# An LSTM inside a two-layer kernel: one tile and one transpose per gate, direct sigmoid and tanh, the cell as a scan, and work around it moved

## The chip, the cores and the metric

The kernel runs on one core of a Trainium2 chip. Its time is the device time of one execution in microseconds, shown as the median of several runs. One execution more was taken with the hardware profiler. The engines are named as the profile names them: PE (TensorE matmuls), PEld (its weight loads), DVE (VectorE), ACT (ScalarE), POOL (GpSimd) and SP (SyncE, which only issues DMAs here). All data is fp32.

## The reference

Two layers, each of an attention-like block and a feed-forward-like block with residual additions, on x of 8 sequences (B) of 512 steps (S) and 256 features (D). The first layer's second block begins with an LSTM, whose outputs go into a routed attention. What the change touches is this LSTM, with H = 256 and all 8 sequences run side by side:

```python
xW = jnp.einsum('ntd,dg->ntg', x, Wx) + b          # 256 -> 4 * 256
def step(carry, xw_t):
    prev_h, prev_c = carry
    a = xw_t + prev_h @ Wh
    i = jax.nn.sigmoid(a[:, :Hdim])
    f = jax.nn.sigmoid(a[:, Hdim:2 * Hdim])
    o = jax.nn.sigmoid(a[:, 2 * Hdim:3 * Hdim])
    g = jnp.tanh(a[:, 3 * Hdim:])
    next_c = f * prev_c + i * g
    next_h = o * jnp.tanh(next_c)
    return ((next_h, next_c), next_h)
```

The states h of all steps are kept, and their mean over the steps enters a router. Other blocks used below: the first layer's attention with a sum over 32768 edges (the "edge stage"); its gated output ("gating"), which makes the LSTM's input x; and "adaptive weights", a product of a hidden vector with a 256 x 8192 matrix for the second layer.

## The kernel before

**Stages.** In order of time: attention of the first layer, the edge stage (to about 446 us), the LSTM loop (464 to 1695 us), routed attention, the second layer's attention, and a second recurrence (a plain tanh RNN, L1419 to L1440) with a mixture of experts beside it.

**One LSTM step** (`lstm`, from L599, the loop from L669). States are kept transposed: features on 128 partitions, two halves k, 8 sequences, so that h is a 128x8 stationary operand. The 1024 gate columns are laid out by the host (`gates`) as four blocks j of 256, each of 64 columns for i, f, g, o. Block j's product lands on partitions 32j to 32j+7 of PSUM tiles: `pgi` (64 columns of i and 64 of f), `pgg` and `pgo`, each in two buffers that alternate by step.

- PE, L677: for each of the three tiles 8 matmuls (2 halves x 4 blocks) add h Wh to what the tile holds.
- PE, L657 (`seed`): right behind them, 12 matmuls put xW of the next step into the other buffers: the stationary operand picks 8 rows of `xw`, a 128x1024 tile of 16 steps x 8 sequences.
- DVE, L683 and L687: three 32x32-block transposes of PSUM tiles into `G`, of 128, 64 and 64 columns.
- ACT, L684 and L688: tanh of i and f together, of g, of o. Sigmoid is written as a tanh: the weights and the bias of i, f and o are halved beforehand (L592 to L595), h is kept doubled, and the cell doubled as well; the DVE operations and the scale of the last tanh make up for it:

```python
STT(pr[:, 1], X[:, 1], 1.0, X[:, 3], ALU.add, ALU.mult)
STT(pr[:, 0], X[:, 0], 1.0, X[:, 2], ALU.add, ALU.mult)
STT(X[:, 3], pr[:, 1], 0.5, pr[:, 0], ALU.mult, ALU.add)
nc.scalar.activation(th, X[:, 3], AF.Tanh, scale=0.5)
STT(ring[:, t % RB], to, 1.0, th, ALU.add, ALU.mult)
```

These are L690, L691, L693 (DVE), L695 (ACT) and L696 (DVE). L696 writes h of the step into `ring`, a tile of 8 steps with two buffers. The next step's L677 waits for it.

**Work between the steps.** The loop is under a manual schedule: PE, ACT and DVE execute in the order in which the code issues, POOL and SP are placed by the scheduler. Behind each step, by its position `at` = t mod 16, a piece of other work is issued:

- `rest`, the generator `gating` (L523 to L553), one of its 8 pieces in positions 15 and 0 to 6. It makes x of 16 steps for a later chunk: two matmuls to `pv` and an addition (L534, L535) in positions 15 and 0, two copies with bias on ACT and two additions (L538, L539) in 1, then products, a tanh and a square (L542, L544, L545, L547, L549), and the result (L552) in 6. `pv` is a single PSUM buffer of the pool `a_pv`.
- `extra`, the generator `adaptive_weights` (L1071 to L1090), in positions 1, 2, 3: a matmul to `pw`, a second one, then the addition of a 8x512 row (L1088) and the DMA of the result. There are 16 rounds of three pieces, in the first 16 chunks. `pw` uses the same PSUM buffer as `pv`. SP loads weights and bias rows ahead (L1080, L1082).
- `project` (L634 to L648): from position 6, two copies on POOL (L639), then eight matmuls (L645) and four additions (L647) give `xw` of the next chunk, through one PSUM buffer.
- every 8 steps: a sum over the 8 states (L708, DVE) and, on POOL, L709, the copy of the 8 states to `hT` times 0.5.

**Before the loop.** In the edge stage (`Edges.sums`), for each of 32 groups DVE makes one-hot tiles (L457, L477) and PE multiplies with them (L468, transposes L485, L489). After its second group `lstm_weights` loads Wx, Wh and the bias (Wh on ACT's queue) and scales them on DVE (L592 to L595); the groups 4, 6 and 8 each let gating take a piece. Then six more pieces follow (L573), then the first `project`, the first seed and the loop. Router (L774): the mean of h with the factor 0.5 / S.

Of the kernel before, what the change touches and what calls it, by code (L numbers as in the profile page):

```python
# [509 lines left out]
def l0_attention(K, es, states):  # L510
# [44 lines left out]
    with ExitStack() as e1:  # L555
# [8 lines left out]
        with ExitStack() as e2:  # L564
            enc0 = K.pool(e2, "a_wv").tile([P, 2, S], F32, name="enc0")
            nc.vector.tensor_tensor(enc0, denseT[:, :, 0, :], xgT, ALU.add)
            with tc.manual_schedule(engines=ORDERED):
                for g, _ in enumerate(edges.sums(enc0, e2, alpha)):
                    if g == 1:
                        weights = lstm_weights(K, lw)  # L570
                    if g in (4, 6, 8):
                        next(rest)
    for _ in range(6):  # L573
        next(rest)
    return hT, rest, weights, pp

# [4 lines left out]
def lstm_weights(K, wp):  # L581

    nc, inp = K.nc, K.inp

    wx = load_kp(nc, wp, inp["lstm_wx"], "wx", 1024)
    wh = load_kp(nc, wp, inp["lstm_wh"], "wh", 1024, eng=nc.scalar)
    bias = wp.tile([P, 1024], F32, name="bias")
    nc.sync.dma_start(out=bias, in_=inp["lstm_b"].partition_broadcast(P))
    for t, f, fg in ((wx, 0.5, None), (bias, 0.5, None), (wh, 0.25, 0.5)):
        t5 = t if t is bias else t.rearrange("p k n -> p (k n)")  # L590
        t5 = t5.rearrange("p (j g n) -> p j g n", g=4, n=64)
        nc.vector.tensor_scalar(t5[:, :, 0:2, :], t5[:, :, 0:2, :], f, None, ALU.mult)  # L592
        nc.vector.tensor_scalar(t5[:, :, 3, :], t5[:, :, 3, :], f, None, ALU.mult)
        if fg is not None:
            nc.vector.tensor_scalar(t5[:, :, 2, :], t5[:, :, 2, :], fg, None, ALU.mult)  # L595
    return wx, wh, bias


def lstm(K, hT, rest, weights, extra):  # L599

    nc, inp = K.nc, K.inp
    ident, xT = K.ident, K.xT  # L610
    mm = nc.tensor.matmul
    STT = nc.vector.scalar_tensor_tensor
    XB = GT
    RB = 8
    with ExitStack() as es:
        wp = K.pool(es, "l_w")
        sp = K.pool(es, "l_s", 3)
        rp = K.pool(es, "l_r", 2)
        xp = K.pool(es, "l_xw", 2)
        psx = K.pool(es, "l_px", 1, PSUM)  # L620
        psg = K.pool(es, "l_pg", 1, PSUM)
        wx, wh, bias = weights
        h0 = wp.tile([P, 2, B], F32, name="h0")
        nc.vector.tensor_scalar(h0, K.h0T, 2.0, None, ALU.mult)
        pick = ident.rearrange("p (b t) -> p t b", b=B)

        pgi = [psg.tile([P, 2, 64], F32, name=f"pgi{i}") for i in range(2)]
        pgg, pgo = [[psg.tile([P, 64], F32, name=f"{n}{i}") for i in range(2)] for n in ("pgg", "pgo")]
        for t in (*pgi, *pgg, *pgo):
            nc.vector.memset(t, 0.0)  # L630
        X = sp.tile([P, 4, 2, B], F32, name="X", tag="X")
        nc.vector.memset(X[:, 3], 0.0)

        def project(t0):  # L634

            xw = xp.tile([P, 1024], F32, name="xw", tag="xw")
            xc = xp.tile([P, 2, P], F32, name="xc", tag="xc")
            for k in range(2):
                nc.gpsimd.tensor_copy(xc[:, k].rearrange("p (b t) -> p b t", b=B), xT[:, k, :, t0 : t0 + XB])  # L639
            yield xw  # L640
            for n in range(4):
                c = slice(n * 256, n * 256 + 256)
                px = psx.tile([P, 256], F32, name="px", tag="px")
                for k in range(2):
                    mm(px, xc[:, k], wx[:, k, c], start=(k == 0), stop=(k == 1))  # L645
                    if k == 1:
                        nc.vector.tensor_tensor(xw[:, c], px, bias[:, c], ALU.add)  # L647
                    yield  # L648

        def parts(t):  # L650

            return (pgi[t % 2], 0, 128), (pgg[t % 2], 128, 192), (pgo[t % 2], 192, 256)

        def seed(t, xw):
            for dst, lo, hi in parts(t):
                for j in range(4):
                    mm(dst[32 * j : 32 * j + B], pick[:, t % XB, :], xw[:, j * 256 + lo : j * 256 + hi], start=True, stop=False)  # L657

        proj = project(0)
        xw = next(proj)  # L660
        for _ in proj:
            pass
        proj = iter(())
        nxt = None
        ring = None
        seed(0, xw)
        E = mybir.EngineType
        es.enter_context(K.tc.manual_schedule(engines={E.PE, E.Activation, E.DVE}))
        for t in range(S):  # L669
            if t % RB == 0:  # L670
                last = ring
                ring = rp.tile([P, RB, 2, B], F32, name="ring", tag="ring")
            for dst, lo, hi in parts(t):
                for k in range(2):
                    hp = h0[:, k, :] if t == 0 else (ring[:, t % RB - 1, k] if t % RB else last[:, RB - 1, k])
                    for j in range(4):
                        mm(dst[32 * j : 32 * j + B], hp, wh[:, k, j * 256 + lo : j * 256 + hi], start=False, stop=(k == 1))  # L677
            if t + 1 < S:
                if t % XB == XB - 1:
                    xw = nxt  # L680
                seed(t + 1, xw)
            G = sp.tile([P, 4, 2, 32], F32, name="G", tag="G")
            nc.vector.transpose(G[:, 0:2].rearrange("p g k b -> p (g k b)"), pgi[t % 2].rearrange("p g n -> p (g n)"))  # L683
            nc.scalar.activation(X[:, 0:2], G[:, 0:2, :, 0:B], AF.Tanh)  # L684
            to = sp.tile([P, 2, B], F32, name="to", tag="to", bufs=2)
            for g, ps, th in ((2, pgg[t % 2], X[:, 2]), (3, pgo[t % 2], to)):
                nc.vector.transpose(G[:, g].rearrange("p k b -> p (k b)"), ps)  # L687
                nc.scalar.activation(th, G[:, g, :, 0:B], AF.Tanh)  # L688
            pr = sp.tile([P, 2, 2, B], F32, name="pr", tag="pr")
            STT(pr[:, 1], X[:, 1], 1.0, X[:, 3], ALU.add, ALU.mult)  # L690
            STT(pr[:, 0], X[:, 0], 1.0, X[:, 2], ALU.add, ALU.mult)  # L691
            X = sp.tile([P, 4, 2, B], F32, name="X", tag="X")
            STT(X[:, 3], pr[:, 1], 0.5, pr[:, 0], ALU.mult, ALU.add)  # L693
            th = sp.tile([P, 2, B], F32, name="th", tag="th")
            nc.scalar.activation(th, X[:, 3], AF.Tanh, scale=0.5)  # L695
            STT(ring[:, t % RB], to, 1.0, th, ALU.add, ALU.mult)  # L696
            at = t % XB
            if at < 7 or at == XB - 1:
                next(rest, None)
            if 0 < at < 4:  # L700
                next(extra, None)
            if at == 6 and t - 6 + XB < S:
                proj = project(t - 6 + XB)
                nxt = next(proj)
            elif at > 6:
                next(proj, None)
            if t % RB == RB - 1:
                nc.vector.tensor_reduce(K.hpart[:, t // RB], ring.rearrange("p t k b -> p k b t"), AX.X, ALU.add)  # L708
                nc.gpsimd.tensor_scalar(  # L709
                    hT[:, :, :, t - RB + 1 : t + 1], ring.rearrange("p t k b -> p k b t"), 0.5, None, ALU.mult  # L710
                )
        for _ in extra:
            pass

# [32 lines left out]
def routed_heads(K, hT, T):  # L747
# [4 lines left out]
    with ExitStack() as es:  # L752
# [18 lines left out]
        for k in range(2):  # L771
            mm(pl, hsum[:, k, :], wr[:, k, :], start=(k == 0), stop=(k == 1))
        lg = wp.tile([B, NH], F32, name="lg")
        nc.vector.scalar_tensor_tensor(lg, pl, 0.5 / S, br, ALU.mult, ALU.add)  # L774
        nm = wp.tile([B, 1], F32, name="nm")
        sm = wp.tile([B, 1], F32, name="sm")
        nc.vector.tensor_reduce(nm, lg, AX.X, ALU.max, negate=True)
# [293 lines left out]
def adaptive_weights(K, wd, hT, pp):  # L1071

    nc, inp = K.nc, K.inp
    mm = nc.tensor.matmul
    with ExitStack() as es:
        sp = K.pool(es, "d_s", 2)
        for n in range(16):
            c = slice(n * S, (n + 1) * S)
            w2 = sp.tile([P, 2, S], F32, name="w2")
            nc.sync.dma_start(out=w2, in_=inp["ada_w2"][:, c].rearrange("(k p) n -> p k n", p=P))  # L1080
            b2 = sp.tile([B, S], F32, name="b2")
            nc.sync.dma_start(out=b2, in_=inp["ada_b2"][c].partition_broadcast(B))  # L1082
            pw = pp.tile([P, S], F32, name="pw", tag="pv")[0:B, :]
            for k in range(2):
                mm(pw, hT[:, k, :], w2[:, k, :], start=(k == 0), stop=(k == 1))
                yield
            ws = sp.tile([B, S], F32, name="ws")
            nc.vector.tensor_tensor(ws, pw, b2, ALU.add)  # L1088
            nc.sync.dma_start(out=wd[:, c], in_=ws)
            yield  # L1090


class Attention:
# [764 lines left out]
def two_layers_kernel(tc, *args):  # L1858
    inp, out = dict(zip(NAMES, args)), args[-1]
    with ExitStack() as es:  # L1860
        K = State(tc, inp, es)
        with tc.tile_pool(name="wd", bufs=1, space=DRAM) as dp, ExitStack() as eh:
# [11 lines left out]
            with ExitStack() as e0:  # L1874

                adaptive_hidden(K, gT)
                hT, rest, weights, pp = l0_attention(K, e0, states)
                lstm(K, hT, rest, weights, adaptive_weights(K, wd, gT, pp))
            el.close()
            with ExitStack() as e1:  # L1880
                T = Layer1(K, e1, wd)
# [19 lines left out]
def lay_out(i):  # L1901
# [10 lines left out]

    def gates(w):
        w = w.reshape(w.shape[:-1] + (4, 4, 64))
        return w[..., [0, 1, 3, 2], :, :].swapaxes(-2, -3).reshape(w.shape[:-3] + (1024,))

    def rank_major(w):
        w = w.reshape(w.shape[:-1] + (4, D, 8)).swapaxes(-1, -2)
# [99 lines left out]
```

## Time and profile before

| | |
|---|---|
| median of 10 runs | 4071.5 us (4061.75 to 4076.65) |
| the profiled execution | 4066.82 us, span of its instructions 4065.0 us |
| mean granted clock of TensorE | 0.967 |
| busy share of the span | PE 87%, PEld 60%, DVE 58%, ACT 37%, POOL 15% |
| LSTM loop, first to last h | 464.55 to 1694.76 us, 511 intervals, mean 2.407 us |
| matmuls in a step | 24 of h Wh, 12 of the seed; each shows as two in the trace |

How to read it: times are counted from the span's start. PE's busy share counts matmuls whose ends are modelled and which overlap, so a high share does not say that PE is full. A line such as "ACT X L684 <- DVE G L683: 658.9, 511, 2.3" says that ACT's instruction of line 684 stood idle for DVE's of line 683: in total, how often, the longest. In a timeline a bracket gives the idle time ahead of an instruction and what released it. Lines are those of the kernel before.

### The profile page before, as it was taken

To read this page: it belongs to the slowest core of one execution; us is meant where nothing else is said; L and a number is where in the kernel's file an instruction comes from. 1 tells how busy PE (TensorE), PEld (TensorE's weight loads), DVE (VectorE), ACT (ScalarE), POOL (GpSimd) and SP (SyncE) were. 2 spreads that over 40 slices of the span, in tenths; PEclk is the share of its full clock that TensorE was granted. 3 is DMA by queue.
4 is the path that set the end of the run, shared out by engine and by line. 5 is a ranking of instruction groups with operands and counts; after the bars stand their busy time and mean duration, and the time that the engine had idled before them with its cause. 6 is when DMAs were issued, how large, how long until landed. Compare 5 with 4: busy or idle time off the path is not lost.

```text
span 4065.0 us, 150864 instructions
## 1 busy us (share of the span) xinstructions
PE 3516.3 (87%) x65188; PEld 2440.4 (60%) x65188; DVE 2350.3 (58%) x8838; ACT 1509.0 (37%) x5341; POOL 606.4 (15%) x1250
## 2 busy tenths in 40 slices
PE   8999888888878888599988999999998797999884
PEld 5533466666666666466656666666666565767564
DVE  4488566666666666467656666666666433333332
ACT  3111233333333333255544444444444322333242
POOL 1010000000000000111022222222222121030412
PEclk9899999999999999899999999999999997999897
DMA  3111000000000000200000000000000122443476
GB/s 106 43 67 69 23 21 21 15 21 15 5 4 4 4 4 4 76 25 25 1 2 2 1 1 2 1 2 1 1 1 1 36 75 69 125 149 102 133 246 202
DMA packets 104842, 173.14 MB, mean 43 GB/s; under 512 B 12576, under 2 KB 71872, under 8 KB 103792
## 3 DMA queue, kind: packets, MB, share of 16 engines
q1 hardware_dynamic: 79792, 114.23, 9.0%
q0 software_dynamic: 12064, 34.34, 2.5%
q10 hardware_dynamic: 12320, 14.94, 1.1%
q8 instruction: 511, 8.37, 0.9%
q14 instruction: 155, 1.27, 0.1%
HBM read 124.53 MB, written 40.10 MB: 40 GB/s over the span
## 4 chain that ended last, share of the span: by engine, by line
PE 44%; DVE 6%; ACT 4%; DMA 2%; issue 1%; SPq 0%; ACTq 0%; POOL 0%; DVEq 0%; POOLq 0%
PE pg L1435 5%; PE pe L1231 4%; PE pt L1274 3%; PE pp L1191 3%; PE po L1289 3%; PE pg L1657 3%; PE px L1306 3%; ACT sm L1251 2%; PE pv L1211 2%; DMA x<-xs 2%; PE pe L893 2%; PE pp L869 1%; PE po L930 1%; PE pt L915 1%; PE py L1673 1%
## 5 line engine op out<-in xcount | busy, mean ns | idle before, releaser
L677 PE MATMUL pgi<-wh,ring 128*8 128x128 f32 x8176 | 325.3, 274 | 209.7 <-DVE ring L696 209.2
L677 PEld LDWEIGHTS pgi<-wh,ring 128*8 128x8 f32 x8176 | 173.9, 89 | 377.2 <-DVE ring L696 366.1
L684 ACT ACTIVATE X<-G 128x32 f32<-128x32 f32 x512 | 117.3, 229 | 671.9 <-DVE G L683 671.9
L1440 DVE STREAM_TRANSPOSE ring<-h 128x64 f32<-128x64 f32 x512 | 125.5, 245 | 396.3 <-ACT h L1439 383.3
L1251 ACT ACTIVATE sm<-sm,nm 128x388 f32<-128x388 f32 (+3 forms) x512 | 284.0, 556 | 175.6 <-DVE nm L1247 175.2
L683 DVE STREAM_TRANSPOSE G<-pgi 128x128 f32<-128x128 f32 x512 | 161.9, 316 | 258.8 <-PE pgi L677 258.7
L1439 ACT ACTIVATE h<-pg 128x64 f32<-128x64 f32 x512 | 114.2, 223 | 456.8 <-PE pg L1435 420.8
L1191 PE MATMUL pp<-hn,wqkv 128*128 128x512 f32 x512 | 243.1, 619 | 30.7 <-ACT oT L1290 29.8
L1435 PE MATMUL pg<-wh,ring 128*8 128x64 f32 x8176 | 221.8, 229 | 52.8 <-DVE ring L1440 49.6
L1274 PE MATMUL pt<-ident,sm 128*128 128x128 f32 x1280 | 191.2, 281 | 75.3 <-DVE sm L1257 62.6
L1274 PEld LDWEIGHTS pt<-ident,sm 128*128 128x128 f32 x1280 | 147.9, 143 | 157.5 <-issue 96.1
L1276 ACT COPY eT<-pt 128x512 f32<-128x512 f32 (+1 forms) x192 | 105.4, 549 | 346.8 <-PE pt L1274 345.4
L1258 POOL COPY pme<-sm 128x4 f32<-128x4 f32 x512 | 119.7, 234 | 754.2 <-DVE sm L1257 750.0
L1435 PEld LDWEIGHTS pg<-wh,ring 128*8 128x8 f32 x8176 | 122.9, 91 | 162.2 <-DVE ring L1440 132.8
L677 PE MATMUL pgo<-wh,ring 128*8 128x64 f32 x8176 | 209.7, 219 | 1.9 <-issue 1.9
L677 PE MATMUL pgg<-wh,ring 128*8 128x64 f32 x8176 | 211.1, 219 | 0.0
L657 PE MATMUL pgi<-xw,ident 128*8 128x128 f32 x4096 | 209.5, 273 | 0.0
L1247 DVE CUSTOM_DVE_ANT_0 sm<-pe,mask 128x260 f32<-128x260 f32 (+2 forms) x384 | 141.9, 425 | 90.3 <-PE pe L1231 89.7
L645 PE MATMUL px<-wx,xc 128*128 128x256 f32 x512 | 181.4, 438 | 5.5 <-POOL xc L639 5.0
L1191 PEld LDWEIGHTS pp<-hn,wqkv 128*128 128x128 f32 x512 | 94.7, 195 | 145.8 <-issue 97.0
L1657 PE MATMUL pg<-xT,w 128*128 128x128 f32 x992 | 172.0, 299 | 10.6 <-DVE a L1520 8.9
L1257 DVE TENSOR_SCALAR sm<-sm,rc 128x388 f32<-128x388 f32 (+3 forms) x512 | 175.9, 386 | 9.0
(505 smaller groups left out, 8044.6 us busy)
## 6 DMA issues: line engine op xcount, KB each, us to landing
w<-in_experts_dram SPq DMA_DIRECT2D x124, 384.0 KB
cb<-order POOLq DMA_DIRECT2D x32, 512.0 KB, 3.9
x<-xs SPq DMA_DIRECT2D x124, 128.0 KB
ys<-y SPq DMA_DIRECT2D x124, 128.0 KB
xs<-zero ACTq DMA_DIRECT2D x2, 4736.0 KB
w<-in_ada_w_dram SPq DMA_DIRECT2D x16, 512.0 KB
w<-in_moh_w_dram SPq DMA_DIRECT2D x32, 192.0 KB
out_dram<-acc SPq DMA_DIRECT2D x32, 128.0 KB
```

Of the source, the lines that this page charges most:

```text
L645: mm(px, xc[:, k], wx[:, k, c], start=(k == 0), stop=(k == 1))
L657: mm(dst[32 * j : 32 * j + B], pick[:, t % XB, :], xw[:, j * 256 + lo : j * 256 + hi], start=True, stop=False)
L677: mm(dst[32 * j : 32 * j + B], hp, wh[:, k, j * 256 + lo : j * 256 + hi], start=False, stop=(k == 1))
L683: nc.vector.transpose(G[:, 0:2].rearrange("p g k b -> p (g k b)"), pgi[t % 2].rearrange("p g n -> p (g n)"))
L1191: mm(pp, T.wqkv[:, k, 0 : 2048].rearrange("p (i g h n) -> p i g h n", i=2, g=4, h=2)[:, i, g, h], self.hn[b][:, k, :], start=(k == 0), sto ...
L1231: mm(pe[a][:, 0 : w - lo], q[r, h, at], k[r, h, lo:w], start=(h == 0), stop=(h == 1))
L1247: nc.vector.tensor_tensor_reduce(out=sm[a][:, lo:w], in0=pe[a][:, 0 : w - lo], in1=T.mask[:, S - n + lo : 4 + S], scale=-1.0 / 8.0, scalar ...
L1251: nc.scalar.activation(sm[a][:, 0:w], sm[a][:, 0:w], AF.Exp, bias=nm[:, a : a + 1], scale=-1.0, accum_out=su[:, a : a + 1])
L1257: nc.vector.tensor_scalar(sm[a][:, 0:w], sm[a][:, 0:w], rc[:, a : a + 1], None, ALU.mult)
L1274: nc.tensor.transpose(pt[:, at, :], sm[i * m + a][:, 4 + j * P : 4 + (j + 1) * P], K.ident)
L1435: mm(pg[32 * j : 32 * j + B], hp, M.wh[:, k, 64 * j : 64 * j + 64], start=False, stop=(k == 1))
L1657: mm(pg, W[m][:, k * D + g * P : k * D + (g + 1) * P], X[m][:, k, :], start=(k == 0), stop=(k == 1))
```

## The change

The change gives each gate its own tile and transpose, uses sigmoid directly, and moves pieces of the other work.

- `gates` orders the columns f, i, g, o. The PSUM tiles are `pgf` and `pgi`, with one buffer each (the same tile in even and odd steps), and `pgg` and `pgo` with two. Each has 64 columns: 32 matmuls of 64 columns for h Wh and 16 for the seed.
- For each gate: a transpose, then sigmoid (f, i, o) or tanh (g) on ACT. i goes to the odd columns of `left`, g to the even columns of `right`. f times the old cell is issued between g's transpose and o's, into the odd columns of `right`.
- The seed of the next step is issued behind the transposes instead of ahead of them.
- The cell is one scan over 32 columns, state = left * state + right: even columns of `left` are 0, so an even column gives g, and the odd column after it i * g + f * c.
- h and the cell are no longer doubled: the scaling in `lstm_weights`, the doubled start state and the factors in the copy to `hT` and in the router go. The copy to `hT` is on ACT.
- The first `project` uses two PSUM buffers in turn (its own and the one of `pv` and `pw`); one gating piece is issued behind the first seed instead of ahead of the projection.
- `adaptive_weights` has four pieces per round, the addition and its row in two halves, and is called in positions 3, 4, 9 and 11.

```diff
@@ l0_attention
-    for _ in range(6):
+    for _ in range(5):
         next(rest)
@@ lstm_weights
-    for t, f, fg in ((wx, 0.5, None), (bias, 0.5, None), (wh, 0.25, 0.5)):
...
-        nc.vector.tensor_scalar(t5[:, :, 0:2, :], t5[:, :, 0:2, :], f, None, ALU.mult)
-        nc.vector.tensor_scalar(t5[:, :, 3, :], t5[:, :, 3, :], f, None, ALU.mult)
-        if fg is not None:
-            nc.vector.tensor_scalar(t5[:, :, 2, :], t5[:, :, 2, :], fg, None, ALU.mult)
     return wx, wh, bias
@@ lstm, ahead of the loop
-        pgi = [psg.tile([P, 2, 64], F32, name=f"pgi{i}") for i in range(2)]
+        pgf, pgi = [[psg.tile([P, 64], F32, name=n)] * 2 for n in ("pgf", "pgi")]
         pgg, pgo = [[psg.tile([P, 64], F32, name=f"{n}{i}") for i in range(2)] for n in ("pgg", "pgo")]
...
+        NC = 2 * B
+        lefts, rights, cells = [[wp.tile([P, 2 * NC], F32, name=f"{n}{i}") for i in range(3)] for n in ("left", "right", "cell")]
+        for t in (*lefts, *rights, *cells):
+            nc.vector.memset(t, 0.0)
+
+        def odd(w, n=1):
+            return w.rearrange("p (k b two) -> p two k b", k=2, two=2)[:, n]
+
-        def project(t0):
+        def project(t0, pools=(psx,)):
...
-                px = psx.tile([P, 256], F32, name="px", tag="px")
+                px = pools[n % len(pools)].tile([P, S], F32, name="px", tag=("px", "pv")[n % len(pools)])[:, 0:256]
...
-            return (pgi[t % 2], 0, 128), (pgg[t % 2], 128, 192), (pgo[t % 2], 192, 256)
+            return [(pg[t % 2], 64 * n, 64 * n + 64) for n, pg in enumerate((pgf, pgi, pgg, pgo))]
...
-        proj = project(0)
+        proj = project(0, (psx, pp))
...
         seed(0, xw)
+        next(rest)
@@ lstm, the step
+            left, right, cell, was = lefts[t % 3], rights[t % 3], cells[t % 3], cells[(t - 1) % 3]
+            sf = sp.tile([P, 2, B], F32, name="sf", tag="sf")
+            so = sp.tile([P, 2, B], F32, name="so", tag="so", bufs=2)
+            for n, (to, f) in enumerate(((sf, AF.Sigmoid), (odd(left), AF.Sigmoid), (odd(right, 0), AF.Tanh), (so, AF.Sigmoid))):
+                G = sp.tile([P, 2, 32], F32, name="G", tag=f"G{n}")
+                nc.vector.transpose(G.rearrange("p k b -> p (k b)"), parts(t)[n][0])
+                nc.scalar.activation(to, G[:, :, 0:B], f)
+                if n == 2:
+                    TT(odd(right), sf, odd(was), ALU.mult)
             if t + 1 < S:
                 if t % XB == XB - 1:
                     xw = nxt
                 seed(t + 1, xw)
-            G = sp.tile([P, 4, 2, 32], F32, name="G", tag="G")
-            nc.vector.transpose(G[:, 0:2].rearrange("p g k b -> p (g k b)"), pgi[t % 2].rearrange("p g n -> p (g n)"))
-            nc.scalar.activation(X[:, 0:2], G[:, 0:2, :, 0:B], AF.Tanh)
...
-            STT(pr[:, 1], X[:, 1], 1.0, X[:, 3], ALU.add, ALU.mult)
-            STT(pr[:, 0], X[:, 0], 1.0, X[:, 2], ALU.add, ALU.mult)
...
-            STT(X[:, 3], pr[:, 1], 0.5, pr[:, 0], ALU.mult, ALU.add)
+            nc.vector.tensor_tensor_scan(cell, left, right, 0.0, ALU.mult, ALU.add)
             th = sp.tile([P, 2, B], F32, name="th", tag="th")
-            nc.scalar.activation(th, X[:, 3], AF.Tanh, scale=0.5)
-            STT(ring[:, t % RB], to, 1.0, th, ALU.add, ALU.mult)
+            nc.scalar.activation(th, odd(cell), AF.Tanh)
+            TT(ring[:, t % RB], so, th, ALU.mult)
             at = t % XB
             if at < 7 or at == XB - 1:
                 next(rest, None)
-            if 0 < at < 4:
+            if at in (3, 4, 9, 11):
                 next(extra, None)
...
-                nc.gpsimd.tensor_scalar(
-                    hT[:, :, :, t - RB + 1 : t + 1], ring.rearrange("p t k b -> p k b t"), 0.5, None, ALU.mult
-                )
+                nc.scalar.copy(hT[:, :, :, t - RB + 1 : t + 1], ring.rearrange("p t k b -> p k b t"))
@@ routed_heads
-        nc.vector.scalar_tensor_tensor(lg, pl, 0.5 / S, br, ALU.mult, ALU.add)
+        nc.vector.scalar_tensor_tensor(lg, pl, 1.0 / S, br, ALU.mult, ALU.add)
@@ adaptive_weights
-            nc.vector.tensor_tensor(ws, pw, b2, ALU.add)
-            nc.sync.dma_start(out=wd[:, c], in_=ws)
-            yield
+            for h in range(2):
+                hs = slice(h * 256, h * 256 + 256)
+                nc.vector.tensor_tensor(ws[:, hs], pw[:, hs], b2[:, hs], ALU.add)
+                if h == 1:
+                    nc.sync.dma_start(out=wd[:, c], in_=ws)
+                yield
@@ lay_out, gates
-        return w[..., [0, 1, 3, 2], :, :].swapaxes(-2, -3).reshape(w.shape[:-3] + (1024,))
+        return w[..., [1, 0, 3, 2], :, :].swapaxes(-2, -3).reshape(w.shape[:-3] + (1024,))
```

More of the change, by code (lines that the diff above doesn't have):

```diff
@@ L588, in lstm_weights, with lstm @@
     nc.sync.dma_start(out=bias, in_=inp["lstm_b"].partition_broadcast(P))
-    for t, f, fg in ((wx, 0.5, None), (bias, 0.5, None), (wh, 0.25, 0.5)):
-        t5 = t if t is bias else t.rearrange("p k n -> p (k n)")
-        t5 = t5.rearrange("p (j g n) -> p j g n", g=4, n=64)
-        nc.vector.tensor_scalar(t5[:, :, 0:2, :], t5[:, :, 0:2, :], f, None, ALU.mult)
-        nc.vector.tensor_scalar(t5[:, :, 3, :], t5[:, :, 3, :], f, None, ALU.mult)
-        if fg is not None:
-            nc.vector.tensor_scalar(t5[:, :, 2, :], t5[:, :, 2, :], fg, None, ALU.mult)
     return wx, wh, bias
-def lstm(K, hT, rest, weights, extra):
+def lstm(K, hT, rest, weights, extra, pp):
     nc, inp = K.nc, K.inp
@@ L611, in lstm @@
     mm = nc.tensor.matmul
-    STT = nc.vector.scalar_tensor_tensor
+    TT = nc.vector.tensor_tensor
     XB = GT
@@ L622, in lstm @@
         wx, wh, bias = weights
-        h0 = wp.tile([P, 2, B], F32, name="h0")
-        nc.vector.tensor_scalar(h0, K.h0T, 2.0, None, ALU.mult)
         pick = ident.rearrange("p (b t) -> p t b", b=B)
-        pgi = [psg.tile([P, 2, 64], F32, name=f"pgi{i}") for i in range(2)]
+        pgf, pgi = [[psg.tile([P, 64], F32, name=n)] * 2 for n in ("pgf", "pgi")]
         pgg, pgo = [[psg.tile([P, 64], F32, name=f"{n}{i}") for i in range(2)] for n in ("pgg", "pgo")]
-        for t in (*pgi, *pgg, *pgo):
+        for t in (pgf[0], pgi[0], *pgg, *pgo):
             nc.vector.memset(t, 0.0)
-        X = sp.tile([P, 4, 2, B], F32, name="X", tag="X")
-        nc.vector.memset(X[:, 3], 0.0)
-        def project(t0):
+        NC = 2 * B
[5 more added lines that the diff above has]
+        def project(t0, pools=(psx,)):
             xw = xp.tile([P, 1024], F32, name="xw", tag="xw")
@@ L674, in lstm @@
                 for k in range(2):
-                    hp = h0[:, k, :] if t == 0 else (ring[:, t % RB - 1, k] if t % RB else last[:, RB - 1, k])
+                    hp = K.h0T[:, k, :] if t == 0 else (ring[:, t % RB - 1, k] if t % RB else last[:, RB - 1, k])
                     for j in range(4):
                         mm(dst[32 * j : 32 * j + B], hp, wh[:, k, j * 256 + lo : j * 256 + hi], start=False, stop=(k == 1))
+            left, right, cell, was = lefts[t % 3], rights[t % 3], cells[t % 3], cells[(t - 1) % 3]
[7 more added lines that the diff above has]
+                    TT(odd(right), sf, odd(was), ALU.mult)
             if t + 1 < S:
@@ L681, in lstm @@
                 seed(t + 1, xw)
-            G = sp.tile([P, 4, 2, 32], F32, name="G", tag="G")
[L683 to L689, printed above, removed]
-            STT(pr[:, 1], X[:, 1], 1.0, X[:, 3], ALU.add, ALU.mult)
-            STT(pr[:, 0], X[:, 0], 1.0, X[:, 2], ALU.add, ALU.mult)
-            X = sp.tile([P, 4, 2, B], F32, name="X", tag="X")
-            STT(X[:, 3], pr[:, 1], 0.5, pr[:, 0], ALU.mult, ALU.add)
+            nc.vector.tensor_tensor_scan(cell, left, right, 0.0, ALU.mult, ALU.add)
             th = sp.tile([P, 2, B], F32, name="th", tag="th")
-            nc.scalar.activation(th, X[:, 3], AF.Tanh, scale=0.5)
-            STT(ring[:, t % RB], to, 1.0, th, ALU.add, ALU.mult)
+            nc.scalar.activation(th, odd(cell), AF.Tanh)
+            TT(ring[:, t % RB], so, th, ALU.mult)
             at = t % XB
@@ L1877, in two_layers_kernel @@
                 hT, rest, weights, pp = l0_attention(K, e0, states)
-                lstm(K, hT, rest, weights, adaptive_weights(K, wd, gT, pp))
+                lstm(K, hT, rest, weights, adaptive_weights(K, wd, gT, pp), pp)
             el.close()
```

## Prediction

> **What bounds the kernel now.** First the table of stages (columns: stretch, length, busy time of PE, its weight loads, DVE, ACT, POOL, then granted clock, DMA share, GB/s).
>
> ```profile
> 446.00:465.00 19.00, 13.32 (x126) 8.43 (x128) 6.72 (x26) 2.50 (x8) 0.52 (x2) 0.73 0.18 58
> 465.00:1695.00 1230.00, 997.83 (x37568) 791.90 (x37558) 796.11 (x4058) 447.98 (x2168) 57.37 (x128) 1.00 0.05 15
> ```
>
> The LSTM takes 1230 of the span's 4065.0 us, and no engine is full in it: it is a chain of 512 steps. The waits of that stretch say who hands on to whom.
>
> ```profile
> ACT X L684 <- DVE G L683: 658.9, 511, 2.3
> ...
> DVE ring L696 <- ACT th L695: 148.6, 511, 0.7
> ACT th L695 <- DVE X L693: 88.8, 506, 0.3
> PEld pw L1085 <- ACT v L538: 21.0, 16, 1.3
> ```
>
> Then one quiet step in order of time (start, duration, instruction).
>
> ```profile
> 907.87 0.62 PE L677 MATMUL pgi<-wh,ring 128*8 128x128 f32 x16 [0.83 <-DVE ring L696]
> ...
> 908.31 0.41 PE L677 MATMUL pgg<-wh,ring 128*8 128x64 f32 x16
> ...
> 908.53 0.41 PE L677 MATMUL pgo<-wh,ring 128*8 128x64 f32 x16
> 908.56 0.32 DVE L683 STREAM_TRANSPOSE G<-pgi 128x128 f32<-128x128 f32 x1 [0.41 <-PE pgi L677]
> ...
> 908.80 0.23 DVE L687 STREAM_TRANSPOSE G<-pgg 128x64 f32<-128x64 f32 x1
> ...
> 909.07 0.22 ACT L688 ACTIVATE X<-G 128x16 f32<-128x16 f32 x1
> ...
> 909.32 0.18 DVE L691 SCALAR_TENSOR_TENSOR pr<-X 128x16 f32<-128x16 f32 x1
> ...
> 909.53 0.18 DVE L693 SCALAR_TENSOR_TENSOR X<-pr 128x16 f32<-128x16 f32 x1
> 909.74 0.22 ACT L695 ACTIVATE th<-X 128x16 f32<-128x16 f32 x1 [0.17 <-DVE X L693]
> 909.99 0.17 DVE L696 SCALAR_TENSOR_TENSOR ring<-to,th 128x16 f32<-128x16 f32 x1 [0.28 <-ACT th L695]
> ...
> 910.21 0.62 PE L677 MATMUL pgi<-wh,ring 128*8 128x128 f32 x16 [0.83 <-DVE ring L696]
> ```
>
> Counted from the first matmul at 0, the chain is: g's matmuls end at 0.85, its transpose starts at 0.93, g's tanh at 1.20, i times g at 1.45, cell 1.66, tanh of the cell 1.87, h 2.12, next matmul 2.34. It runs through **g**, not through the wide i,f transpose at 0.69. Over all 511 intervals between starts of L696, 412 are 2.33 to 2.35, 60 are 2.41 or 2.42, 16 are 2.62 or 2.63, 16 are 3.50 or 3.51, and seven others add 5.1 together: 511 x 2.343 + 60 x 0.075 + 16 x 0.28 + 16 x 1.165 + 5.1 = 1230.
>
> **The step, part by part.**
>
> PE: four gates of 64 columns instead of 128, 64, 64. The second and third groups show the price: pgg to pgo is 0.22, and pgi's two gates take 0.44, the same. A 64-column group ends 0.41 after its start and DVE follows 0.07 later, so transposes can start at 0.48 (f), 0.70 (i), 0.92 (g), 1.14 (o). G is not earlier than now.
>
> DVE and ACT ahead of g: transposes of 64 columns can follow each other at 0.13 (904.15 and 904.28 behind a late start), another operation follows one at 0.17 (the scan at 3384.80 behind 3384.63). f's sigmoid runs 0.76 to 0.98, so f times cell, queued behind g's transpose, starts at 0.92 + 0.17 = 1.09 without waiting; o's transpose behind it at about 1.23. Now g's sequel is unchanged: tanh at 1.20, the scan at 1.45. DVE is free for it at about 1.40, so f times cell costs nothing; the cover is 0.05.
>
> The scan replaces i times g and the cell sum, two dependent hops of 0.21 (L691 to L693, L693 to L695), by one. Its only row is 16 elements:
>
> ```profile
> L1583 DVE TENSOR_TENSOR_SCAN end<-ones,nt x4: 148/159/191, 3384.8 to 3888.5; 128x16 f32<-128x16 f32 x4
> ```
>
> With 16 elements more at 1.04 ns each (128 elements 285 ns at L535, 256 take 418 at L549) it takes 0.176, and with 0.035 to the next engine the hop is 0.21. From below: the shortest scan, 0.148, and h at the 137 ns of L1492 instead of 176 take 0.07 off the step. From above: if all 159 ns grew with the elements, 0.318, 0.14 more. I take the slope's value, as it comes from operations of the same engine and sizes around it.
> [...]
>
> ACT runs five functions instead of four: o's sigmoid starts at 1.23 + 0.25 + 0.03 = 1.51, and the tanh of the cell can follow 0.13 to 0.16 later (908.91 to 909.07), at 1.67 at the latest; the scan releases it at 1.66. Changing between sigmoid and tanh needs no table load: the later recurrence alternates L1493 and L1666 (sigmoid) with L1439 (tanh) behind a single load of 1283 ns. A strided write of 16 elements has no row; bounds 0 to the 0.01 that 32 elements cost over 16 (229 against 217), taken 0.
>
> New step: 1.45 + 0.21 + 0.25 + 0.22 = 2.13, and I take **2.15** for the two covers of 0.05 and 0.01. 511 x (2.343 - 2.15) = **98.6 saved**.
>
> The seeds of the next step now follow the transposes, as f and i have one PSUM tile each, without a second: f's transpose ends at 0.73, before PE is through with four gates (0.88); i's at 0.95, where PE comes to it at 0.99. Nothing, unless DVE is late. Projection matmuls start at 1.44 (918.76 after 917.32), have 0.43 of issue and end before 2.13.
>
> Other work on DVE must fit between h and the transposes. Now h to the wide transpose is 0.92; then it is 0.70, but f's transpose may be 0.18 late before g's is touched. The longest items (0.49 at L552, 0.28 and 0.36 at L535 and L708) end 0.58 to 0.66 after h. Nothing.
>
> **Pieces moved.** In 16 steps the first adaptive matmul waits on PE for the bias copies of the same step, with the next step's gates queued behind it:
>
> ```profile
> 896.70 0.61 ACT L538 ACTIVATE v<-pv,cols 128x128 f32<-128x128 f32 x2
> ...
> 897.36 0.60 PE L1085 MATMUL pw<-w,gT 128*8 128x512 f32 x1 [1.14 <-ACT v L538]
> ```
>
> Moved from position 1 to 3, it finds the copies long done: 16 x 1.165 = **18.6 saved**. What is late next is PE: two such matmuls per 16 steps start at 1.38 and issue for 0.86, to 2.24, 0.09 after the new step's end: 32 x 0.085 = 2.7 lost. The one addition of 0.67 (L1088) behind the 0.42 of L545 made the 2.62 steps; halves of about 0.42 in otherwise empty positions 9 and 11 fit: 16 x 0.28 = **4.5 saved**. SP's DMA of the result leaves 8 positions (17 us) later; SP's queue holds the next bias row and weight block behind it, which issue a whole chunk, 34 us, ahead of use.
>
> **State copy to ScalarE.** The 60 long steps of 2.41 are those whose h opens a ring buffer and waits for POOL's read as well. On ACT the copy (L1648 has 266 ns for 128x128) falls into 0.98 of idle time ahead of f's sigmoid, and its wait is the same engine's as h's. 60 x 0.075 = **4.5 saved**.
>
> **Weights no longer scaled.** This is in the edge stage, and DVE does stand there for a DMA with PE behind it:
>
> ```profile
> 203.94 0.69 DVE L592 TENSOR_SCALAR wh<-wh 128x1024 f32<-128x1024 f32 x1 [7.02 <-DMA wh<-in_lstm_wh_dram]
> ...
> 205.91 6.57 PE L489 MATMUL U<-or,kg 128*64 128x512 f32 x16 [4.80 <-DVE or L477]
> ```
>
> From one group's transposes on PE to the next it is 200.45 to 215.84, 15.4; the next ones are 7.6 (215.84 to 223.44), PE's own work. DVE would begin L477 at 195.4 instead of 205.2. Bounds 4.8 (the idle time shown) and 7.8; I take **7.0 saved**, near the difference of like intervals, less something for transfers.
>
> **Start and end.** Four projections, each waiting for the addition before it, take 451.7 to 462.3 at a clock of 0.73. With two banks the second overlaps; the gating matmuls (0.6) now stand behind them: about **2.0 saved**. Two table loads are added, 1.28 each, one behind gating at 450, one behind the last copy at 1695 while DVE's L769 runs 1.83: nothing, 2.6 if bare. The twelve memsets before the loop fall into DVE's waits of 1.1 to 4.2 there.
>
> **Sum.** 98.6 + 18.6 - 2.7 + 4.5 + 4.5 + 7.0 + 2.0 = 132.5 saved. The profiled execution took 4066.82 (span 4065.0); the median of the runs, 4071.5, is 4.7 above it. 4071.5 - 132.5 = **3939 us**.
>
> **Rivals.**
> 1. The forecast, step 2.07 to 2.20: 3898 to 3965. Chance 0.66.
> 2. DVE's queue closes last: if f times cell and o's transpose each follow at 0.21, the spacing of dependent operations, o's transpose is at 1.35, the scan at 1.56 to 1.59, step up to 2.29: 3965 to 4011. For it: covers of 0.05 and less. Against: spacing of 0.13 and 0.17 in rows that do not depend on each other. The upper price of the scan ends here too. Chance 0.20.
> 3. The change does not shorten the step: another gate ends last at 2.34. Then 34 remain (the other savings): 4037. For it only that two covers fail at once. Chance 0.06.
> 4. Slower: PE's clock. The stretch before the loop shows 0.73, and 0.66 of the chain (three gates' issue at 0.22) grows with it. At 0.73 the step is 2.15 + 0.24 = 2.39: 4064, no change; from 0.71 down, where the growth of 0.27 eats 132.5 / 511 = 0.26, the kernel is slower, at 0.65 4120. Against: 1.00 now, with more idle time in each step. Chance 0.06, a third of it no change.
> The last 0.02 is below 3898.
>
> Range 3900 to 4010: cases 1 and 2, which leaves out 0.14; the bounds of the scan, 3898 and 4010, are its ends. A difference of 0.2% is about what can be told from none. Faster 0.94 (cases 1 to 3 and the last), same 0.02 and slower 0.04 (case 4).
>
> **What would show it.** Intervals between h of 2.13 to 2.17 and none at 3.5, 2.62 or 2.42; the scan about 0.18 long, starting 1.45 after the first matmul with ACT's tanh of g as its releaser; the tanh of the cell released by the scan, not by o's sigmoid; no DVE idle for wh near 200. A scan released by DVE itself, or over 0.25 long, would be rival 2; a granted clock under 0.9 in the LSTM, rival 4.

## The result and the profile after

The kernel after takes 4247.8 us (median of 8 runs, 4234.7 to 4253.2) against 4070.6 for the kernel before (median of 28 runs): a ratio of 1.0434, 95% interval 1.0425 to 1.0443. It is slower where 3939 was forecast. Its profiled execution has a span of 4248.6 us, 183.6 more than before.

First the table of stages of the kernel after, in the columns and stretches of before.

```profile
446.00:465.00 19.00, 16.37 (x708) 12.60 (x710) 11.48 (x55) 8.07 (x36) 0.00 (x0) 1.00 0.11 32
465.00:1695.00 1230.00, 936.57 (x43033) 718.94 (x43021) 718.96 (x3531) 526.86 (x2368) 14.90 (x56) 1.00 0.04 11
```

The granted clock of the loop is 1.00 as before. ACT alone is fuller, 527 us instead of 448 in 1230; PE's busy time has fallen from 998 to 937 us. But the counts in brackets say that PE executes 43,033 matmuls and 43,021 weight loads where it had 37,568 and 37,558, and it isn't through: the loop ends at 1877.5. From first to last h it takes 451.3 to 1877.5, 1426.2 us against 1230.2, a step of 2.791 on the mean against 2.407. So the account is: loop 196.0 more, start 13.2 less, the rest 0.9 more, together 183.7.

The waits of the same stretch (engine, line, releaser: total, times, longest):

```profile
ACT sf L682 <- DVE G L681: 504.8, 441, 2.7
...
PEld pgo L675 <- issue: 56.0, 56, 2.4
...
PEld pgg L675 <- issue: 51.3, 54, 2.2
PEld pgf L675 <- issue: 45.5, 105, 1.6
...
PEld pgg L654 <- issue: 30.2, 27, 2.0
```

Rows like the last four are new in this size. (The wait of pw for ACT, 21.0 before, is gone.) "Issue" says that PE stood still, for up to 2.4 us, and that the profile shows no instruction that it waited for. The largest such row of before was this:

```profile
PEld pgi L677 <- issue: 10.7, 33, 0.3
```

and 32 of its 33 waits are of another kind: they lie in position 1, two in each of 16 chunks, where only the next weight loads stand, while PE executes the 512-column matmul of the adaptive weights (L1085).

Two steps in order of time show both sides of the result (start, duration, instruction):

```profile
905.87 0.41 PE L675 MATMUL pgf<-wh,ring 128*8 128x64 f32 x16
...
906.79 0.25 DVE L681 STREAM_TRANSPOSE G<-pgg 128x64 f32<-128x64 f32 x1
...
907.08 0.22 ACT L682 ACTIVATE right<-G 128x16 f32<-128x16 f32 x1
...
907.33 0.23 DVE L689 TENSOR_TENSOR_SCAN cell<-left,right 128x32 f32<-128x32 f32 x1
...
907.59 0.22 ACT L691 ACTIVATE th<-cell 128x16 f32<-128x16 f32 x1
907.84 0.18 DVE L692 TENSOR_TENSOR ring<-so,th 128x16 f32<-128x16 f32 x1 [0.28 <-ACT th L691]
...
908.08 0.28 PE L675 MATMUL pgf<-wh,ring 128*8 128x64 f32 x5
...
909.37 0.34 PE L675 MATMUL pgf<-wh,ring 128*8 128x64 f32 x10 [1.01 <-issue]
...
911.98 0.28 PE L675 MATMUL pgg<-wh,ring 128*8 128x64 f32 x3
...
913.11 0.34 PE L675 MATMUL pgg<-wh,ring 128*8 128x64 f32 x11 [0.86 <-issue]
```

In lines of the kernel after: L675 is a gate's product, L654 the seed, L681 a transpose, L689 the scan. The first step is almost the forecast's: g's transpose 0.92 after the first matmul, g's tanh 1.21, scan 1.46, tanh of the cell 1.72, h 1.97, next matmul 2.21 (2.15 was forecast). In the next, PE stops in the middle of f's group of 16, for 1.01, and goes on with the same operands. It stops again at 913.11. Between the two restarts the trace holds 128 weight loads and 128 matmuls: 256 instructions in 3.74 us. This holds over the whole loop: of its 308 stops over 0.4 us in which PE neither loads nor multiplies and which are put down to "issue", 224 come 256 PE instructions after the one before, and 68 two or three times 256. In the loop of the kernel before there are two such stops. Of the 511 steps after, 126 are 2.19 to 2.25; the rest spread up to 3.6, few above.

An fp32 matmul shows as two loads and two matmuls, so four instructions of PE. The step had 36 matmuls and now has 48: 192 instructions, and on the mean 3.0 of projections and other pieces (the texts on record below take 3.5). The page's row of the instruction queue agrees, here before and after (packets, MB, share):

```profile
q8 instruction: 511, 8.37, 0.9%
```

```profile
q8 instruction: 607, 9.95, 1.0%
```

96 packets more of 16.4 KB; at 256 instructions each they are 24,576, which is 512 steps x 48 added PE instructions. In 1400 us of the loop:

```profile
465.00:1865.00 1400.00, 1056.96 (x48828) 814.04 (x48816) 812.50 (x3996) 597.82 (x2687) 17.30 (x65) 1.00 0.05 14
```

that is 97,644 PE instructions, 69.7 per us; and 195.0 / 69.7 = 2.80, the mean step.

### The profile page after: what moved, and what is told of

It reads as the page before. It is cut to its first block, busy times and chain, and to the rows that moved or that the text cites. A ratio compares the mean times of both kernels' runs of the same rounds, so it can differ in the third digit from the quotient of the medians.

```text
span 4248.6 us, 176426 instructions
## 1 busy us (share of the span) xinstructions
PE 3589.1 (84%) x77476; PEld 2472.3 (58%) x77476; DVE 2380.2 (56%) x8854; ACT 1675.4 (39%) x5919; POOL 561.6 (13%) x1186
## 4 chain that ended last, share of the span: by engine, by line
PE 75%; issue 8%; DVE 7%; ACT 6%; DMA 2%; SPq 0%; ACTq 0%; POOL 0%; DVEq 0%; POOLq 0%
PE pgf L675 5%; PE pg L1432 5%; PE pe L1228 4%; PE px L642 4%; PE pp L1188 4%; PE pt L1271 3%; PE po L1286 3%; PE pg L1654 3%; PE U L489 3%; PE px L1303 3%; PE pgi L675 3%; PE pk L468 3%; PE pgg L675 3%; PE pgo L675 2%; PE pv L1208 2%
## 5 line engine op out<-in xcount | busy, mean ns | idle before, releaser
L682 ACT ACTIVATE sf<-G 128x16 f32<-128x16 f32 x512 | 110.5, 216 | 591.2 <-DVE G L681 591.2
L675 PE MATMUL pgf<-wh,ring 128*8 128x64 f32 x8176 | 228.7, 220 | 107.1 <-DVE ring L692 78.6
L675 PE MATMUL pgo<-wh,ring 128*8 128x64 f32 x8176 | 240.4, 219 | 50.9 <-issue 50.9
L675 PEld LDWEIGHTS pgf<-wh,ring 128*8 128x8 f32 x8176 | 127.6, 88 | 263.7 <-DVE ring L692 203.1
L675 PE MATMUL pgg<-wh,ring 128*8 128x64 f32 x8176 | 236.3, 219 | 50.6 <-issue 50.6
L675 PE MATMUL pgi<-wh,ring 128*8 128x64 f32 x8176 | 229.8, 219 | 26.7 <-issue 25.6
L681 DVE STREAM_TRANSPOSE G<-pgf 128x64 f32<-128x64 f32 x512 | 128.0, 250 | 205.2 <-PE pgf L675 195.0
L654 PE MATMUL pgf<-xw,ident 128*8 128x64 f32 x4096 | 180.2, 220 | 28.5 <-issue 27.9
L654 PE MATMUL pgo<-xw,ident 128*8 128x64 f32 x4096 | 177.8, 220 | 27.1 <-issue 27.1
L675 PEld LDWEIGHTS pgo<-wh,ring 128*8 128x8 f32 x8176 | 161.6, 90 | 63.6 <-issue 63.6
L654 PE MATMUL pgi<-xw,ident 128*8 128x64 f32 x4096 | 175.8, 222 | 25.9 <-issue 23.1
```

Of the source, the lines that this page charges most:

```text
L681: nc.vector.transpose(G.rearrange("p k b -> p (k b)"), parts(t)[n][0])
```

## Experiments

Theory S: PE's instructions arrive in blocks of 256, at most some 70 per us over a long stretch. The kernel before needs 147.0 / 2.407 = 61 per us and is under that; the kernel after would need 195.0 / 2.20 = 89 and is held to 70. The rivals in the texts on record put the loss on what the change does to the order of waits and to the tiles: W is a wait made by the single buffers of f and i and by the later seed, Z a collision of PE's writes with DVE's reads of the four small tiles. By both a change in the number of matmuls alone should do little.

**Matmuls added to the kernel before, nothing else changed** (n = 4, 8 and 12; the sums are not used):

```diff
@@ seed, ahead of the 12 matmuls
+            for i in range(n):
+                r = slice(32 * (i % 4), 32 * (i % 4) + B)
+                mm(pgo[t % 2][r, 0:8], pick[:, t % XB, :], xw[:, 0:8], start=True, stop=True)
```

They have 8 columns each and stand where PE waits for h. In the text for 4, "the same" is the kernel with 12.

> The same with 4 more matmuls of 8 columns per step, 40 in all. S: 160 + 3.5 instructions need 2.33, just under the quiet step of 2.34, so a little is lost where a step is already late: 4071 to 4100. W and Z: within 5 us of the kernel before.

> The kernel before with 8 extra matmuls of 8 columns per step, ahead of the seed, where PE otherwise waits for h (their sums are not used). Per step 36 + 8 = 44 matmuls, which is 176 PE instructions, and 3.5 others on the mean: 179.5. S (supply of PE's instructions, 70 per us by the kernel after and by the run with 12 added): 179.5 / 70 = 2.56 us for a step where before had 2.407, so 511 x 0.157 = 80 us more, 4150 us. If a step of 8 added matmuls costs two thirds of what 12 cost (a cost for each matmul, from the first on): 4072 + 0.67 x 198 = 4205 us. If 12 are over some limit of the order of the work and 8 are not: within 15 us of before.

> The kernel before with 12 more matmuls of 8 columns per step, ahead of the seed, into a part of the tile of o that the seed then overwrites: 48 matmuls, as the changed kernel has, in time in which PE is idle; nothing else is changed. S: 192 + 3.5 instructions per step need 2.79, so the loop takes 511 x 0.38 = 193 us more, about 4265, with idle time of PE that nothing in the profile explains every 256 instructions. W and Z: 12 x 2 x 0.014 = 0.34 us of PE's idle time, seen only where a long matmul follows, below 15 us in all, about 4080.

| added | PE instructions per step | divided by 70 | mean step | time, ratio (interval) |
|---|---|---|---|---|
| 0 | 147.0 | 2.10 | 2.407 | 4070.6 |
| 4 | 163.0 | 2.33 | 2.421 | 4079.3, 1.0019 (1.0007 to 1.0030) |
| 8 | 179.0 | 2.56 | 2.564 | 4152.8, 1.0212 (1.0195 to 1.0229) |
| 12 | 194.9 | 2.78 | 2.802 | 4269.3, 1.0487 (1.0465 to 1.0510) |
| kernel after | 195.0 | 2.79 | 2.791 | 4247.8, 1.0434 (1.0425 to 1.0443) |

Each ratio is against runs of the kernel before made beside it. By the mean step, the first four added matmuls cost the loop 7 us, the next four 73, the last four 122: no price for each matmul, but a limit, past which four more should cost 16 x 511 / 70 = 117. The run with 12 rebuilds the loss of the change without a new tile, scan, order or function. Its loop and that with 8 (table of stages, two runs):

```profile
465.00:1665.00 1200.00, 969.90 (x41913) 768.53 (x41915) 680.84 (x3419) 378.27 (x1822) 48.10 (x107) 1.00 0.04 11
```

```profile
465.00:1665.00 1200.00, 1010.94 (x42153) 795.12 (x42140) 744.36 (x3751) 414.00 (x2002) 53.09 (x118) 1.00 0.04 11
```

83,828 and 84,293 PE instructions in 1200 us: 69.9 and 70.2 per us, by two step lengths. And the waits of the run with 12 have the new rows:

```profile
PEld pgo L657 <- issue: 69.2, 79, 2.0
...
PEld pgi L680 <- issue: 52.3, 138, 1.9
```

**The supply by itself.** A kernel of 2048 matmuls each of 64, 96, 128 and 256 columns, with no LSTM and no waits:

```diff
+        for n in range(512):
+            for j in range(4):
+                mm(c64[32 * j : 32 * j + 8], w, mv[:, 0:64], start=True, stop=True)
...
```

> Not the reference's work: output of zeros, and four stretches of 2048 matmuls without waits, of 128x8 by 64, 96, 128 and 256 columns, each 8192 instructions of PE, that is 32 times 256. S: about 117 us for each of the first three (32 x 3.65) and 225 for the last (0.055 per pair of instructions). Without a limit of the supply, by 13.75 ns per pair at 64 columns: 56, 84, 113, 225.

It ran once, 576.3 us. Its timeline, two blocks of 64 columns, then two of 96:

```profile
32.99 1.97 PE L57 MATMUL c<-mv,w 128*8 128x64 f32 x128 [1.76 <-issue]
...
36.45 1.97 PE L57 MATMUL c<-mv,w 128*8 128x64 f32 x128 [1.48 <-issue]
```

```profile
126.91 2.83 PE L60 MATMUL c<-mv,w 128*8 128x96 f32 x128 [0.63 <-issue]
...
130.64 2.83 PE L60 MATMUL c<-mv,w 128*8 128x96 f32 x128 [0.90 <-issue]
```

Each row is 128 matmuls and, beside them, 128 loads. Longer matmuls have shorter stops: blocks of either size come every 3.45 to 4.00 us there, and 26 blocks of 64 columns between 25.81 and 120.00 came every 3.62 on the mean, 70.7 instructions per us. PE executes a block of 64 columns in 1.97, which is 130 instructions per us, so this is no price of each instruction: PE stands still until the next block. At 128 columns only 4.7 us of such stops are left in the waits. The four stretches took 119.0, 115.8, 116.3 and 221.3 us, as S expected; without a limit the first two had been put at 56 and 84 (the other two cannot decide it). The page's row of the instruction queue is

```profile
q8 instruction: 128, 2.10, 1.5%
```

128 packets for 32,768 PE instructions, 256 each. From 25 us on the core moves 2 to 5 GB/s, and a packet of 16.4 KB every 3.62 us is 4.5 of them: nothing else is transferred beside them.

**The kernel after with f and i in one tile**: 36 matmuls again, with its scan, direct functions, order and moved pieces.

```diff
-        pgf, pgi = [[psg.tile([P, 64], F32, name=n)] * 2 for n in ("pgf", "pgi")]
+        pgi = [psg.tile([P, 2, 64], F32, name="pgi")] * 2
...
-                nc.vector.transpose(G.rearrange("p k b -> p (k b)"), parts(t)[n][0])
+                nc.vector.transpose(G.rearrange("p k b -> p (k b)"), gates(t)[n])
```

> The changed kernel with one edit: f and i share one tile of 128 columns again (one buffer), so a step has 24 + 12 matmuls instead of 32 + 16; the transposes per gate, the scan, the seed behind the transposes and all moved pieces stay. Theory S (PE's instruction supply): the changed kernel's PE takes 256 instructions between stalls and 3.65 us for each 256, 70 per us; with 144 + 3.5 per step the supply allows 2.10, so the step falls to the chain's 2.19 to 2.25 and the kernel to about 3945. Theory W (a wait made by the single buffers of f and i and by the seed behind the transposes): both are still there, so it stays near 4248. Theory Z (four small tiles collide between PE's writes and DVE's reads): half of the loss goes, about 4100.

4013.5 us, ratio 0.9859 (0.9840 to 0.9879). The stops of PE are gone and the loss has become a gain; W and Z both expected more than that. S missed by 68: steps are 2.24 where PE has no other matmuls, 2.32 in positions 7 to 14 (the projection's), 2.33 in 15 and 0 (gating's) and 2.43 in 3 and 4 of the 16 chunks with adaptive weights. At 2.24, f's transpose and behind it i's start from 0.69 on, as both need the whole tile, and g's at 1.00, 0.08 late. For the longer steps the waits name the single tile:

```profile
PEld pgi L663 <- DVE G L690: 116.7, 488, 0.3
...
DVE xw L644 <- PE px L642: 29.3, 120, 0.7
```

The seed needs both transposes, and the projection is queued on PE behind it.

**The same with two buffers, and the seed ahead of the transposes again:**

```diff
-        pgi = [psg.tile([P, 2, 64], F32, name="pgi")] * 2
+        pgi = [psg.tile([P, 2, 64], F32, name=f"pgi{i}") for i in range(2)]
...
+            if t + 1 < S:
+                if t % XB == XB - 1:
+                    xw = nxt
+                seed(t + 1, xw)
...
-            if t + 1 < S:
-                if t % XB == XB - 1:
-                    xw = nxt
-                seed(t + 1, xw)
```

> The kernel of e1 (f and i in one tile, 36 matmuls) with two buffers for that tile and the seed ahead of the transposes again. In e1 the seed waits for both transposes (0.24 per step), and the steps with a projection take 2.32 where the others take 2.24, since the addition on DVE waits for the projection and the next transposes stand behind it. If that wait is the cause, the projection ends 0.2 earlier, nearly all steps take 2.24, and the kernel about 3985. If the 2.32 is something else, it stays at 4013.

3984.2 us, ratio 0.9789 (0.9767 to 0.9811): faster than both kernels, and as expected (its two edits were not separated). 469 of the 511 steps are 2.24 or 2.25, the mean is 2.267, and the largest stop left is this:

```profile
PEld pgo L663 <- issue: 4.5, 16, 0.5
```

71,505 PE instructions in 1100 us are 65.0 per us, under the limit.

**Four tiles with a shorter seed.** The kernel after with its four tiles, single buffers and order, but one seed matmul of 128x128 weights per gate instead of four of 128x8: 36 matmuls. xW is laid out for it by 16 DMAs per chunk, and the projection is issued earlier, in larger pieces.

```diff
-                for j in range(4):
-                    mm(dst[32 * j : 32 * j + B], pick[:, t % XB, :], xw[:, j * 256 + lo : j * 256 + hi], start=True, stop=False)
+                mm(dst, pick[:, t % 4, :], xw[:, t % XB // 4, lo:hi], start=True, stop=False, skip_group_check=True)
...
+                if at in (7, 8, 10):
+                    next(proj, None)
```

> The changed kernel with its four tiles, single buffers for f and i, scan and order, but with the seed of a gate as one matmul (weights 128x128 that pick 8 rows for each of the four blocks; xW is laid out for it by 16 small DMAs per 16 steps, and the projection is issued 3 steps earlier): 32 + 4 matmuls, 36 in all. S: 147.5 instructions per step allow 2.10. Eight weight loads of 128 columns take about 1.0 where the seed took 0.55, so steps with a projection are held by PE at about 2.4, the others at 2.19: 511 x 2.32 = 1186, about 4010. W or Z (both still as in the changed kernel, and PE busier): 4248 or more.

4135.4 us, ratio 1.0157 (1.0133 to 1.0180). The total missed S's 4010 by far: steps with two projection pieces last 2.9 to 3.75. PE also loads eight 128-column weights there (0.30 for two), and in position 10 the second piece waits up to 0.9 for DVE's addition, which frees the buffer. But 238 of the 511 steps are 2.19 or 2.20, at 58 PE instructions per us over the loop, and the largest row of stops has none over 0.3 us:

```profile
PEld pgf L686 <- issue: 43.2, 138, 0.3
```

These, too, are weight loads alone, in positions with other matmuls ahead of them.

So the order and the single buffers of the change allow 2.19 for step after step once PE has fewer instructions; that refutes W and Z as what holds the steps at 2.79. As a kernel it is no remedy.

**Single parts.** The run with one tile for f and i, with the scan replaced:

```diff
-            nc.vector.tensor_tensor_scan(cell, left, right, 0.0, ALU.mult, ALU.add)
+            ig = sp.tile([P, 2, B], F32, name="ig", tag="ig")
+            TT(ig, odd(left), odd(right, 0), ALU.mult)
+            TT(odd(cell), ig, odd(right), ALU.add)
```

> The kernel of e1 with the scan replaced by a product i g and an addition of f c (two DVE operations that depend on each other). If the scan is on the chain and saves one hop, the step grows by a hop of 0.21 less the scan's excess over a product of 0.05: 511 x 0.16 = 82, about 4095. If another gate ends last, no change: 4013.

4057.3 us, ratio 0.9968 (0.9951 to 0.9985), so 44 more than with the scan. Steps are 2.39 almost everywhere: 0.15 over the quiet 2.24, but only 0.07 over the 2.32 of the projection steps, which another chain had set. The expectation had taken 2.24 for all of them.

And the kernel before with the moved pieces alone:

```diff
-            if 0 < at < 4:
+            if at in (3, 4, 9, 11):
...
-            nc.vector.tensor_tensor(ws, pw, b2, ALU.add)
-            nc.sync.dma_start(out=wd[:, c], in_=ws)
-            yield
+            for h in range(2):
+                hs = slice(h * 256, h * 256 + 256)
+                nc.vector.tensor_tensor(ws[:, hs], pw[:, hs], b2[:, hs], ALU.add)
+                if h == 1:
+                    nc.sync.dma_start(out=wd[:, c], in_=ws)
+                yield
```

> The kernel before with the adaptive pieces alone moved (positions 3, 4, 9, 11, the addition in halves). By the prediction's terms 18.6 + 4.5 saved, and no loss by the matmul of 512 columns, as the step keeps its 2.34: about 4048. If the wait only moves: 4071.

4043.4 us, ratio 0.9928 (0.9908 to 0.9948). Where there were 16 steps each of 3.50 and of 2.62, five over 2.6 are left; the 2.41 steps of positions 7 and 15 remain.

## Why the prediction was wrong

- **The step that failed** is "PE: four gates of 64 columns instead of 128, 64, 64", which found "the same" for PE. It compared how long PE executes, 0.22 for each 64 columns, and that was right: g's transpose starts at the forecast 0.92. But the 12 more matmuls of a step were counted in columns, not in instructions. At 70 per us, 195.0 instructions take 2.79, which sets the step whatever the chain of gates does. The sum for the step was 98.6 saved; the loop lost 196.0. The rate of before could be read from the counts in brackets, 75,126 in 1230 us, 61 per us. The limit could not: that loop has but two of the stops, and it was the trace's densest long stretch (the second recurrence needs 46 per us).
- **The rival for slower** had the right engine and the wrong cause. It made the clock fall below 0.71; the clock was 1.00.
- **The chain beside PE** was right but for the scan. It lasts 225 ns in the median where the slope gave 176, within the bounds of 148 and 318:

```profile
L689 DVE TENSOR_TENSOR_SCAN cell<-left,right x512: 180/225/326, 450.8 to 1877.0; 128x32 f32<-128x32 f32 x171
```

  Undisturbed steps are therefore 2.19 to 2.21, not 2.15; on 511 steps some 25 us. The prediction's row of 16 elements held scans of two kinds, and its median of 159 mixed them. Those that start while a transpose on DVE still runs take 148 with 16 elements (3384.80 and 3545.34, before) and 180 to 185 with 32 (65 of the 512, after); those that start when DVE is through take 191 (3888.47, before) and mostly 225. (The fourth of before, 170, starts under another operation's end.) The scan of the chain is of the second kind, as it waits for g's tanh. The added 16 elements cost 32 to 37 ns in the first kind (median 34) and 34 in the second, not the slope's 16 x 1.04 = 17. f times cell cost nothing in the step shown above, and DVE's queue (rival 2) didn't close last: the scan follows g's tanh.
- **Pieces moved**: 18.6 + 4.5 forecast, 25 measured alone (the interval allows 21 to 37), 21.8 of them in the loop. **State copy**: in the best version the 2.41 steps of positions 7 and 15 are gone, with a median of 2.24 like the others; the copy takes 410 ns on ACT, not the 266 of the row taken for it, and is covered all the same.
- **Weights and start**: the loop starts 13.2 earlier, 9.0 forecast. The one-hot group that had waited for wh now goes on without a stop:

```profile
195.47 3.65 PE L468 MATMUL pk<-oc,k 128*64 128x512 f32 x16
...
199.64 3.65 PE L489 MATMUL U<-or,kg 128*64 128x512 f32 x16
```

  From that stage's first one-hot products at 187.62 (186.41 after) to its last products, L501 at 445.61 (436.43 after), 8.0 are saved, 7.0 forecast, and 4.0 from there to the second step, 2.0 forecast. 1.2 lie ahead of it and have no cause in the change that the trace shows.

With the failed step replaced by the supply, the sum holds: what the pieces and the copy save inside the loop is hidden by it, and 4071.5 + (511 x 2.79 - 1230.2) - 9.0 = 4258, against 4247.8; 4.2 of the rest is the earlier start. The 70 per us in it were read from the kernel after itself; with the 70.7 of the kernel of matmuls alone, 2.76 per step, the sum is 4243.

## What to carry to other kernels

Count the instructions that PE needs per us in the tightest loop, not only its busy time: here it got no more than 70 to 71 per us, and an fp32 matmul is four of them, however few columns it has (8 to 256 here). A tile split in two doubles the matmuls for the same columns, so merge columns, and split only the evictions (the best version keeps four transposes and four functions on three tiles). Idle time of PE put down to "issue" in the middle of a group, at multiples of 256 instructions (292 of the 308 stops here), is the sign; rows of weight loads alone, behind a long matmul (none over 0.3 us here), are not.

## What the runs showed of the hardware

- PE was supplied 256 instructions mostly every 3.45 to 4.0 us, a few blocks up to 6.2, in the LSTM and in a kernel of nothing else; without a stop it executes a 64-column fp32 matmul's four instructions in 1.97 / 64 = 0.031 us. The 256 were counted between two stops, and the page of the kernel of matmuls alone has 128 packets for 32,768 PE instructions. The loop of the kernel after would need 89 per us, was held to 70, and got 196 us longer.
- A rate near the limit cost little here: 67.3 per us (4 added) lengthened the loop by 7 us, and 65.0 (the best version) has stops of 4.5 us in its largest row.
- What sets the 3.6 us per block stays open: no run changed the supply itself.
